# A four-part sequence network on one core: the scan's sum over states by accumulated transposes, exp/ln table loads placed after planning, and a re-planned issue order

## Chip, cores and metric

The kernel runs on one core of one Trainium2 chip. The metric is the device time of one execution in microseconds (us). The kernel before takes 1695.54 us (median of 3 runs, 1694.59 to 1696.02).

## What is computed

Eight sequences of 256 tokens with 128 features go through six stages: a gated linear recurrence, local attention with a gated feed-forward block (two layers) and a selective scan ("mamba"), a mixture of 32 experts, a block of chunked attention and feed-forward layers, a mixture of 8 experts, and a last attention layer with a ternary linear map. All of it is float32, each stage with residual and normalisation. The part that the change rewrites is the selective scan, cut to its core:

```python
xz = x @ W_in;  x_inner, z = jnp.split(xz, 2, axis=-1)
xc = silu(causal_conv(x_inner));  x_ssm = xc @ W_xproj      # delta, B (16 states), C (16 states)
delta = softplus(x_ssm[..., :1] * w_dt + b_dt);  A = -exp(A_log)
# h_t = exp(delta*A) * h_(t-1) + delta*B*xc ;  y = sum over the 16 states of h * C
y = selective_scan(xc, delta, A, B, C) + xc * D_param
out = (y * silu(z)) @ W_out
```

## The kernel before

Activations lie with the 128 features on the partitions and tokens along the free axis. `_Kernel` emits the six stages as Python generators, stage by stage: `rglru`, `local_mamba`, `moe1`, `chunked`, `moe2`, `typed`. What sets the order of the work is `_Order`, at the very end: it takes all instructions and their dependencies, runs a list scheduler over five queues (PE, ACT, DVE, POOL, SP) with a table of durations (`LENGTHS`: time until the queue is free, time until the result is there), and in `impose` chains every queue in the order found. A ready instruction is chosen by its rank, which is its place in the program plus an entry of the table `BIAS` (by queue, tile and stage). `STAY` is a handicap for an instruction that needs another ACT table set or another PE tile shape than the one before. So a change in an instruction, in a duration or in a bias can move instructions on all queues in all stages.

**The scan of one sequence** (`mamba_sequence`, L1216 to L1327). The 256 inner channels are two halves `c` of 128 partitions. PE makes `xin` and `z`; ACT applies Silu to `z` (tile `sz`, L1244) and, after DVE's convolution, to `xc` (L1245). Then come `xps`, a broadcast row `raw`, ACT's softplus steps (L1273 to L1276), and POOL (DVE in the last sequence) makes `e`, `r`, `d` and `u = d*xc` (L1280 to L1284). Eight steps `m` follow, each with two of the 16 states:

- SP loads the rows of B and C, spread over the partitions (`bc`, L1262); ACT makes four `da = exp(d*na)` (L1295);
- DVE makes `hs = u*B` (L1297), scans it in place (L1299) and multiplies it by C (L1300), each over 128x1024 elements;
- PE adds both states' halves up in one PSUM bank `y` by two matmuls with the identity as weights and 128x512 moving columns (L1303). On this line the trace lists the helper `mm`, L863; each float32 matmul leaves two records.

After the eighth step DVE adds `xc*D` from PSUM (L1306, two instructions), POOL multiplies by `sz` (L1307, tile `t`; DVE in the last sequence), PE multiplies by `wout`, and a layer normalisation and the router's logits follow. Four local-attention sequences and two scans are in flight together. When the last scan runs there is nothing left beside it but the folding of later weights and the routing of the first 14 token tiles.

**The routing of `moe1`** (`route1`, L1468 to L1536) runs once for token tiles 0 to 13, which need sequences 0 to 6, and once for tiles 14 and 15. Its DVE steps end in `put` (L1512), the row numbers. After that POOL scatters each tile's 128 rows to DRAM by an indirect DMA (L1616, 14 and then 2). SP and ACT read the sorted rows back (`got`, L1636) when all 16 scatters have landed, and only then has PE work for the experts.

**ACT table sets.** Exp and Ln share a set; Sigmoid, Gelu and Silu need others. `exp_ln` (L891 to L897) emits an explicit load of the Exp/Ln set in the program, after the last Gelu or Silu of a block, and `keep` ties it to its place. The planner handles that load as an instruction. Where an activation finds another set, the compiler adds a load ahead of it; the trace lists such a load on the activation's own line, and the explicit ones at L893.

Of the kernel before, what the change touches and what calls it, by code (L numbers as in the profile page):

```python
# [23 lines left out]
P = 128  # L24
# [285 lines left out]
class _Order:  # L310
# [12 lines left out]
    STAY = dict(PE=70, ACT=310)  # L323
    BIAS = {
        "ACT  1": 495, "ACT  3": -495, "ACT d 2": -1445, "ACT e 4": -700, "ACT e 6": 370, "ACT fh 4": -30, "ACT four 4": 630, "ACT four 5": -345,
        "ACT ge 2": 385, "ACT got 3": 50, "ACT got 5": 590, "ACT k 2": -275, "ACT kp 4": -40, "ACT lakq 2": -75, "ACT lavp 2": -95, "ACT lg 2": 620,
        "ACT lnrs 1": 225, "ACT lnrs 2": -280, "ACT lnsq 2": 40, "ACT ot 6": 75, "ACT ptsb 2": -740, "ACT qsq 2": -5, "ACT r 2": -70, "ACT rg 1": -590,
        "ACT rg 2": -320, "ACT rn 2": 55, "ACT rs 4": -50, "ACT rs 6": -25, "ACT s 6": -190, "ACT savp 2": -5, "ACT sg 3": 560, "ACT sh 5": -250,
        "ACT spl 1": -410, "ACT spt 1": -15, "ACT st 6": 460, "ACT v 2": 25, "ACT xc 2": -2725, "ACT xchunked 2": -400, "ACT xchunked 4": -390,
        "ACT xs 2": 10, "ACT xsq 4": -660, "DVE ab 4": 720, "DVE bt 3": -1225, "DVE bt 5": 190, "DVE centre 0": -205, "DVE d 2": -10,  # L330
        "DVE decaypart 4": -240, "DVE e 2": 50, "DVE four 5": 105, "DVE fs 4": 10, "DVE gate 2": -345, "DVE gate 5": -320, "DVE get 2": 180, "DVE get 4": 5,
        "DVE get 5": 850, "DVE got 4": -40, "DVE h 2": 5, "DVE h 5": -525, "DVE hs 2": 5, "DVE k 5": -680, "DVE lares 2": -200, "DVE lg 4": 665,
        "DVE nm 2": -135, "DVE nm 6": -95, "DVE oh 2": -285, "DVE oh 4": 2440, "DVE oh 5": -180, "DVE ptsb 2": 20, "DVE ptsb 6": -250, "DVE put 2": 190,
        "DVE put 4": 480, "DVE q 5": 470, "DVE q 6": 785, "DVE r 2": -120, "DVE rc 2": -270, "DVE rc 4": 175, "DVE route 2": -345, "DVE s 2": 20,
        "DVE s 5": -95, "DVE s 6": 1585, "DVE sares 2": 30, "DVE sel 4": -50, "DVE sg 3": -250, "DVE sm 4": 365, "DVE spt 1": 810, "DVE st 6": 150,
        "DVE sum 2": -705, "DVE t 5": 400, "DVE th 4": 650, "DVE u 2": 255, "DVE vec 2": 50, "DVE we 4": -30, "DVE wlocal 2": 1325, "DVE xc 2": -1830,
        "DVE xla 4": -580, "DVE xlf 4": 75, "DVE xlocal 2": -860, "DVE xmoe 6": 10, "DVE xpf 4": -10, "DVE xrglru 2": 205, "DVE xsa 4": 485, "DVE ys 3": 100,
        "DVE z 4": -190, "PE a 2": 50, "PE acc 5": 10, "PE b 2": 30, "PE bt 3": 1010, "PE bt 5": -580, "PE cum 2": 80, "PE cum 4": -1270, "PE fold 2": 105,
        "PE g 2": -700, "PE gate 1": -345, "PE gate 2": 345, "PE hps 4": -15, "PE kps 4": 95, "PE lg 2": 205, "PE lin 6": -1140, "PE ln 1": 355,
        "PE ln 2": -45, "PE o 6": -910, "PE out 4": -35, "PE pg 5": -20, "PE proj 5": 100, "PE proj 6": -570, "PE ps 4": -455, "PE pt 2": -25,  # L340
        "PE pt 4": -125, "PE pu 3": 2550, "PE pu 5": -720, "PE py 3": 740, "PE qkt 2": -1425, "PE raw 2": -1360, "PE rows 2": 585, "PE sc 2": -60,
        "PE sc 4": 30, "PE sc 6": -1215, "PE v 5": 470, "PE v 6": -20, "PE vps 2": 1025, "PE vps 4": -10, "PE wo 2": 60, "PE wo 6": -855, "PE wout 2": -95,
        "PE xps 2": -790, "PE y 2": 20, "PE z 2": 40, "PE zt 4": -20, "POOL biasrows 3": -595, "POOL e 4": 415, "POOL e 6": -305, "POOL got 5": 490,
        "POOL km 5": 665, "POOL mean 0": 635, "POOL one 0": 395, "POOL places 2": -70, "POOL places 5": -240, "POOL q 5": 50, "POOL q 6": -325,
        "POOL rest 4": -990, "POOL rg 1": -25, "POOL rows 4": 85, "POOL ss 2": -20, "POOL t 2": 595, "POOL u 2": 110, "POOL zero 0": -35,
        "POOL zeros 1": -385, "SP bc 2": 200, "SP cst 3": -455, "SP got 3": 535, "SP got 5": 505, "SP outdram 6": 275, "SP places 1": 1460,
        "SP rottable 0": 45, "SP routetables 0": 495, "SP rows 4": -370, "SP scales 2": 40, "SP vec 0": -1475, "SP wattn 2": 15, "SP wmoe 2": -150,
        "SP wmoe 4": -150, "SP wmoe 5": -100, "SP xs 2": -660,
    }
    LENGTHS = {  # L350
        "ACT  LoadActFuncSet  ": (1178, 1283), "ACT d Ln 128x512 128x512": (544, 649), "ACT da Exp 128x255 128x255": (403, 508),
        "ACT e Abs 128x256 128x256": (460, 565), "ACT e Exp 128x128 128x128": (422, 527), "ACT e Exp 128x256 128x256": (460, 565),
        "ACT e Exp 128x512 128x512": (526, 631), "ACT four Exp 128x2 128x2": (98, 203), "ACT got DMACopy 128x512 128x512": (451, 3502),
        "ACT h TensorCopy 64x255 64x255": (295, 400), "ACT k TensorCopy 128x512 128x512": (484, 589), "ACT lnrs Exp 128x256 128x256": (317, 422),
        "ACT lnsq Square 128x256 128x256": (278, 383), "ACT ot TensorCopy 128x512 128x512": (490, 595), "ACT qsq Square 128x512 128x512": (498, 603),
        "ACT r Relu 128x256 128x256": (462, 567), "ACT rg Exp 128x1020 128x1020": (1039, 1144), "ACT rg Ln 128x1024 128x1024": (949, 1054),
        "ACT rn Exp 128x16 128x16": (111, 216), "ACT rn Ln 128x16 128x16": (116, 221), "ACT rs Exp 128x2 128x2": (97, 202),
        "ACT rs Ln 128x2 128x2": (98, 203), "ACT sh Silu 128x512 128x512": (492, 597), "ACT xc Identity 128x256 128x256": (465, 570),
        "ACT xc Silu 128x512 128x512": (524, 629), "ACT xchunked TensorCopy 128x256 128x256": (260, 365), "ACT xmoe Identity 128x256 128x256": (404, 509),
        "ACT xs TensorCopy 33x256 33x256": (255, 360), "ACT xsq Square 128x128 128x128": (296, 401), "DVE biaspart TensorCopy 96x256 96x256": (198, 283),  # L360
        "DVE decay TensorScalarPtr 128x512 128x512": (516, 601), "DVE decaypart TensorCopy 128x512 128x512": (334, 419),
        "DVE four TensorScalarPtr 128x4 128x4": (74, 159), "DVE ge TensorScalarPtr 128x256 128x256": (384, 469),
        "DVE ge TensorScalarPtr 85x256 85x256": (368, 453), "DVE h TensorTensor 128x256 128x256": (317, 402),
        "DVE hs TensorScalarPtr 128x1024 128x1024": (2191, 2276), "DVE hs TensorTensor 128x1024 128x1024": (1123, 1208),
        "DVE mv BNStatsAggregate 128x2 128x6": (85, 170), "DVE nm TensorTensor 128x8 128x8": (67, 152), "DVE ptsb TensorCopy 128x512 128x512": (594, 679),
        "DVE rc Reciprocal 128x16 128x16": (158, 243), "DVE rc Reciprocal 128x4 128x4": (83, 168), "DVE rc Reciprocal 128x8 128x8": (109, 194),
        "DVE rg TensorScalarPtr 128x256 128x256": (580, 664), "DVE rottable TensorScalarPtr 128x256 128x256": (260, 345),
        "DVE s TensorScalarPtr 128x128 128x128": (253, 338), "DVE s TensorTensor 128x256 128x256": (324, 409), "DVE st BNStats 128x6 128x128": (197, 282),
        "DVE sum TensorReduce 128x32 128x448": (736, 821), "DVE t TensorScalarPtr 128x256 128x256": (385, 470),
        "DVE t TensorTensor 128x512 128x512": (595, 680), "DVE vec TensorTensor 128x1 128x1": (60, 145), "DVE vec TensorTensor 85x1 85x1": (59, 144),  # L370
        "DVE vs TensorCopy 128x512 128x512": (594, 679), "DVE wlocal TensorScalarPtr 128x682 128x682": (483, 568),
        "DVE x TensorScalarPtr 128x256 128x256": (369, 454), "DVE xc TensorScalarPtr 128x254 128x254": (384, 469),
        "DVE xla TensorScalarPtr 128x256 128x256": (429, 514), "DVE xlocal TensorTensor 128x256 128x256": (310, 395),
        "DVE xpf TensorScalarPtr 128x256 128x256": (577, 662), "DVE z TensorScalarPtr 128x128 128x128": (292, 377),
# [62 lines left out]
    def group(self, i):  # L437
# [5 lines left out]
        if e == "ACT":  # L443
            return 1 if op == "LoadActFuncSet" else self.SETS.get(str(x.func).split(".")[-1]) if op == "Activation" else None
        return None

    def change(self, i):
        x, e, op = self.ops[i]
        if e == "ACT":
            return 0.0 if op == "LoadActFuncSet" else self.TABLE  # L450
# [120 lines left out]
    def length(self, i):  # L571
# [20 lines left out]
        if e == "ACT":  # L592
            if op == "LoadActFuncSet":
                return float(self.TABLE), float(self.TABLE)
# [1805 lines left out]
```

## Time and profile before

| what | before |
|---|---|
| median of 3 runs | 1695.54 us |
| the profiled execution, and the span of its trace | 1695.66 us, 1692.0 us |
| mean granted TensorE clock | 0.947 |
| PE, PE weight loads | 1442.4 us (85%), 932.5 us (55%) |
| DVE, ACT, POOL | 1138.2 us (67%), 976.5 us (58%), 579.2 us (34%) |
| ACT table loads | 74 of 1283 ns |

The span leaves out 3.66 us around the trace. A busy share is an average over six stages with different limits, so the profile is read here by windows of time: about 0 to 42 us is `rglru`, 42 to 800 us `local_mamba`, to 852 us the hand-over to `moe1` and `moe1` itself, to 1290 us `chunked`, to 1440 us `moe2`, to the end `typed`. The chain of waits is the sequence of work that ended last, followed back from the last instruction; "issue" is time in it in which an engine waited for nothing that the profile shows.

### The profile page before, as it was taken

What the parts mean: (1) busy time and instruction counts of PE and PEld (TensorE: products, weight loads), DVE (VectorE), ACT (ScalarE), POOL (GpSimd) and SP (SyncE); (2) the same over time, 40 slices, a digit from 0 to 9 for tenths busy, and PEclk for the clock granted to TensorE, in tenths of its full rate; (3) what the DMA queues carried; (4) which work ended last, traced back from release to release, by engine and by line L of the source; (5) the groups of instructions that cost most, each with busy time, mean ns of one, the idle gap of its engine ahead of it and who ended that gap; (6) DMA issues with size and microseconds to landing.
All of it is one profiled execution on the core that took longest, in us unless ns stands there. A gap on an engine that the chain in (4) does not pass through costs nothing.

```text
span 1692.0 us, 28693 instructions
## 1 busy us (share of the span) xinstructions
PE 1442.4 (85%) x10858; PEld 932.5 (55%) x10858; DVE 1138.2 (67%) x2182; ACT 976.5 (58%) x2661; POOL 579.2 (34%) x535
## 2 busy tenths in 40 slices
PE   2688897979788877676679999999997998999997
PEld 1355553545454544343557776766674764566664
DVE  5755579898989898689354656566445332588885
ACT  3777887787877868644135554545443222366654
POOL 1344462616263423100331222221214004567573
PEclk7799999999999998899789999999997998999998
DMA  5000012121212213266310000000102121000000
GB/s 193 1 1 1 1 39 63 39 63 39 63 39 63 64 38 97 66 196 242 111 47 2 8 14 11 7 8 5 46 2 68 47 82 30 18 5 4 8 4 10
DMA packets 45113, 77.97 MB, mean 46 GB/s; under 512 B 5580, under 2 KB 21988, under 8 KB 43824
## 3 DMA queue, kind: packets, MB, share of 16 engines
q1 hardware_dynamic: 39648, 70.02, 13.8%
q0 software_dynamic: 3216, 5.07, 1.1%
q8 instruction: 85, 1.39, 0.3%
q10 hardware_dynamic: 2112, 1.05, 0.2%
q14 instruction: 52, 0.43, 0.1%
HBM read 66.87 MB, written 10.76 MB: 46 GB/s over the span
## 4 chain that ended last, share of the span: by engine, by line
PE 49%; DVE 23%; ACT 11%; issue 9%; POOL 5%; DMA 2%; another core or an unknown queue 0%; SPq 0%; ACTq 0%; DVEq 0%; POOLq 0%
PE vps L863 7%; PE kps L863 6%; PE sc L863 5%; PE out L863 4%; DVE hs L1299 3%; DVE hs L1300 3%; PE pu L863 3%; PE pg L863 3%; PE pt L974 3%; DVE hs L1297 2%; PE o L863 2%; ACT e L1146 2%; PE hps L863 2%; PE py L863 2%; PE acc L863 2%
## 5 line engine op out<-in xcount | busy, mean ns | idle before, releaser
L863 PE MATMUL y<-hs,ident 128*128 128x512 f32 x256 | 136.7, 647 | 30.2 <-DVE hs L1300 29.9
L1151 POOL TENSOR_TENSOR e<-e,rc 128x1024 f32<-128x1024 f32 x32 | 79.6, 2486 | 228.3 <-DVE rc L1150 227.6
L1299 DVE TENSOR_TENSOR_SCAN hs<-da,hs 128x1024 f32<-128x1024 f32 x64 | 154.1, 2409 | 0.1
L2250 ACT ACTIVATE e<-sc,nm 128x128 f32<-128x128 f32 (+1 forms) x256 | 105.1, 426 | 64.1 <-DVE nm L2245 55.2
L974 PE MATMUL pt<-ident,e 128*128 128x128 f32 x768 | 119.2, 281 | 18.0 <-POOL e L1151 12.4
L1295 ACT ACTIVATE da<-d,na 128x255 f32<-128x255 f32 x256 | 110.5, 508 | 22.5 <-DVE hs L1299 20.2
L1146 ACT ACTIVATE e<-sc,nm,rn 128x128 f32<-128x128 f32 x256 | 114.7, 468 | 10.9 <-DVE nm L1141 10.5
L974 PEld LDWEIGHTS pt<-ident,e 128*128 128x128 f32 x768 | 88.4, 143 | 56.3 <-issue 19.2
L2253 POOL TENSOR_TENSOR e<-e,rc 128x1024 f32<-128x1024 f32 x48 | 91.1, 1897 | 65.6 <-DVE rc L2252 65.5
L1829 POOL TENSOR_TENSOR e<-e,rc 128x512 f32<-128x512 f32 x32 | 33.9, 1059 | 226.1 <-DVE rc L1828 173.4
L1098 POOL TENSOR_TENSOR t<-t,t 128x512 f32<-128x512 f32 x64 | 84.1, 1316 | 61.1 <-DVE t L1085 56.0
L1651 POOL DMA_INDIRECT got<-ybuf,get x48 | 45.7, 952 | 169.0 <-DMA ybuf<-ys 87.6
L1804 ACT COPY kp<-kps 128x512 f32<-128x512 f32 x128 | 74.8, 585 | 48.5 <-PE kps L863 46.7
L1297 DVE TENSOR_TENSOR hs<-u,bc 128x1024 f32<-128x1024 f32 x64 | 87.5, 1384 | 6.2 <-POOL u L1284 5.5
L863 PEld LDWEIGHTS y<-hs,ident 128*128 128x128 f32 x256 | 47.5, 204 | 77.9 <-DVE hs L1300 47.5
L1300 DVE TENSOR_TENSOR hs<-hs,bc 128x1024 f32<-128x1024 f32 x64 | 87.5, 1369 | 0.0
L863 PE MATMUL qk<-w_local,h 128*128 128x512 f32 x128 | 71.1, 644 | 13.0 <-DVE t L1085 6.2
L976 DVE COPY ptsb<-pt 128x512 f32<-128x512 f32 x104 | 69.0, 677 | 17.0 <-PE pt L974 16.0
L1840 ACT COPY vs<-vps 128x512 f32<-128x512 f32 x64 | 37.4, 584 | 67.5 <-PE vps L863 56.8
L863 PE MATMUL vps<-sa_vp,x_lf 128*32 128x512 f32 x512 | 69.8, 594 | 0.0
L976 ACT COPY ptsb<-pt 128x512 f32<-128x512 f32 x88 | 51.4, 584 | 31.3 <-PE pt L974 30.7
L2245 DVE TENSOR_REDUCE nm<-sc 128x4 f32<-128x1024 f32 (+1 forms) x48 | 58.3, 1215 | 15.2 <-PE sc L863 14.6
(380 smaller groups left out, 3800.0 us busy)
## 6 DMA issues: line engine op xcount, KB each, us to landing
bc<-xs SPq DMA_DIRECT2D x128, 256.0 KB
w_moe<-in_e_dram SPq DMA_DIRECT2D x16, 768.0 KB
w_attn<-in_w_dram SPq DMA_DIRECT2D x4, 1024.0 KB
w_local<-in_w_dram SPq DMA_DIRECT2D x2, 1557.0 KB
places<-zeros SPq DMA_DIRECT2D x2, 1280.0 KB
got<-places SPq DMA_DIRECT2D x6, 256.0 KB
ybuf<-ys SPq DMA_DIRECT2D x8, 160.0 KB
x_in<-in_x_dram SPq DMA_DIRECT2D x1, 1024.0 KB
```

Of the source, the lines that this page charges most:

```text
L863: return self.nc.tensor.matmul(out, lhsT, rhs, start=start, stop=stop)
L974: self.last = self.nc.tensor.transpose(pt[:, j * P : (j + 1) * P], src[:, j * P : (j + 1) * P], self.ident)
L976: copy(sb.rearrange("p a b -> p (a b)"), pt)
L1098: nc.gpsimd.tensor_add(t1, t1, t2)
L1146: nc.scalar.activation(e[:, j, g, :], scs[:, j, g, :], AF.Exp, bias=nm[:, j, g : g + 1], scale=rq[:, j, g : g + 1], accum_out=sm[:, j, g : ...
L1151: nc.gpsimd.tensor_tensor(e, e, rc.unsqueeze(3).to_broadcast([P, 2, 4, P]), ALU.mult)
L1295: nc.scalar.activation(da[:, n, c, 1:S], d[:, c, 1:S], AF.Exp, scale=na[:, i : i + 1])
L1297: nc.vector.tensor_tensor(hs, u.unsqueeze(1).to_broadcast(shp), bn, ALU.mult)
L1299: nc.vector.tensor_tensor_scan(line(hs), line(da), line(hs), 0.0, ALU.mult, ALU.add)
L1300: nc.vector.tensor_tensor(hs, hs, cn, ALU.mult)
L2250: nc.scalar.activation(e[:, i, :], sc[:, i, :], AF.Exp, bias=nm[:, i : i + 1], accum_out=sm[:, i : i + 1])
L2253: nc.gpsimd.tensor_tensor(e, e, rc.unsqueeze(2).to_broadcast([P, n, keys]), ALU.mult)
```

## The change

- **Sum over states.** Each 128x512 identity matmul becomes four 128x128 PE transposes that accumulate in the PSUM bank, so `y` now has tokens on the partitions. Accordingly `z` is made with tokens on the partitions, `xc*D` is made on POOL (in place, after `u`) and enters the sum as four more transposes, one DVE instruction multiplies `y` by `sz`, four transposes (`yg`) turn the product back and ACT copies it to SBUF for `wout`. Over the kernel 128 matmuls become 544 accumulating transposes and 32 ordinary ones.
- **Table loads.** `exp_ln` and `keep` go, and so does the preload of the Silu set in `route1`. The planner plans without loads; when its order is found, one load of the Exp/Ln set is put directly ahead of each Exp or Ln that follows another set.
- **Row writes and gathers.** The planner's duration for an indirect DMA on POOL goes from 995 (`places`) and 949 (`got`) to 1280 ns.
- **The plan.** All `LENGTHS` entries are renewed, `BIAS` is another table throughout, `STAY` goes from PE 70, ACT 310 to PE 140, ACT 720.

```diff
-    STAY = dict(PE=70, ACT=310)
+    STAY = dict(PE=140, ACT=720)
...
-        "POOL got DMACopy 128x128 2560x128": (949, 2493),
-        "POOL places DMACopy 2560x128 128x128": (995, 2277),
+        "POOL got DMACopy 128x128 2560x128": (1280, 2500),
+        "POOL places DMACopy 2560x128 128x128": (1280, 2500),
...
     def impose(self):
         order, _ = self.plan()
+        ring, last = [], None
+        for i in order["ACT"]:
+            g = self.groups[i]
+            if g is not None:
+                if g == 1 != last:
+                    load = self.tc.nc.scalar.preload_act_table_set("natural_log_exp_and_others")
+                    self.ops.append((load.ins, "ACT", "LoadActFuncSet"))
+                    ring.append(len(self.ops) - 1)
+                last = g
+            ring.append(i)
+        order["ACT"] = ring
...
-            for c in range(2):
-                self.mm(ps[:, c * S : (c + 1) * S], win[:, 256 + c * P : 256 + (c + 1) * P], x)
+            for t in range(2):
+                self.mm(ps[:, t * S : (t + 1) * S], x[:, t * P : (t + 1) * P], win[:, 256:512])
             sz = tile("sz", 2)
             nc.scalar.activation(flat(sz), ps, AF.Silu)
-            self.exp_ln(nc.scalar.activation(xc, xc, AF.Silu))
+            nc.scalar.activation(xc, xc, AF.Silu)
...
+            nc.gpsimd.tensor_tensor(xc, xc, self.v("dpar", 0, 2).unsqueeze(2).to_broadcast([P, 2, S]), ALU.mult)
         yield 3.0
-        yp = self.psum("Y", "y")
+        yp = self.psum("Y", "y").rearrange("p (t c d) -> p t c d", t=2, c=2)
+
+        def gathered(src, first, last):
+            for c in range(2):
+                for t in range(2):
+                    self.nc.tensor.matmul(
+                        yp[:, t, c, :], src[:, c, t * P : (t + 1) * P], self.ident, start=first and c + t == 0, stop=last and c + t == 2, is_transpose=True
+                    )
...
             for n in range(2):
-                self.mm(yp, self.ident, flat(hs[:, n]), m == 0 and n == 0, m == 7 and n == 1)
+                gathered(hs[:, n], m == 0 and n == 0, False)
             yield 2.3
-        yg = tile("t")
+        gathered(xc, False, True)
+        nc.vector.tensor_tensor(flat(sz), yp.rearrange("p t c d -> p (t c d)"), flat(sz), ALU.mult)
+        ps = self.psum("M", "yg")
         for c in range(2):
-            nc.vector.scalar_tensor_tensor(yg[:, c, :], xc[:, c, :], self.v("dpar", c), yp[:, c * S : (c + 1) * S], ALU.mult, ALU.add)
-        eng.tensor_mul(yg, yg, sz)
+            for t in range(2):
+                nc.tensor.transpose(ps[:, c * S + t * P : c * S + (t + 1) * P], sz[:, t, c * P : (c + 1) * P], self.ident)
+        nc.scalar.copy(flat(sz), ps)
         ps = self.psum("M", "wout")[:, 0:S]
         for c in range(2):
-            self.mm(ps, wout[:, c, :], yg[:, c, :], c == 0, c == 1)
+            self.mm(ps, wout[:, c, :], sz[:, c, :], c == 0, c == 1)
```

The other hunks drop the calls of `exp_ln` and `keep` (in `rglru_group`, `local_block`, `local_mamba`, `route1`, `moe1`, `moe2`, `typed_weights`) and the planner's cases for a load.

How the order of the instructions moves, from the two built kernels: ACT has 62 table loads instead of 74. Up to the second recurrence group in `local_mamba` there are 8 instead of 13, in the rest of `local_mamba` 48 instead of 55, and 6 in both after that. On DVE, the `put` of the 14 tiles stands behind the last scan and directly ahead of the last `hs` product before; after, DVE still has 3 scans, 5 `hs` products and 3 short routing steps between `put` and the end of the last `hs` product, and behind that product, ahead of the multiplication by `sz`, four routing steps of the 14 tiles and one step of a later weight. ACT's new copy of `sz` stands between the next sequence's convolution start (`xc`, Identity) and its Silu, or directly behind that Silu. In the last two sequences the Exp/Ln load stands after the Abs and Relu of the softplus and ahead of its Exp, where before it followed the Silu directly.

## The prediction

> **What bounds the kernel.** I read the page's first two parts, then busy time by windows, the chain of waits in order of time, and single rows. The page's shares and the matmul group that the change removes:
>
> ```profile
> PE 1442.4 (85%) x10858; PEld 932.5 (55%) x10858; DVE 1138.2 (67%) x2182; ACT 976.5 (58%) x2661; POOL 579.2 (34%) x535
> ...
> L863 PE MATMUL y<-hs,ident 128*128 128x512 f32 x256 | 136.7, 647 | 30.2 <-DVE hs L1300 29.9
> ```
>
> PE leads on average, and the sum over states takes 136.7 us of it. But all of it lies in `local_mamba`, so its worth is read there. The columns after the length are busy us (and counts) of PE, weight loads, DVE, ACT, POOL, then the clock:
>
> ```profile
> 296.00:381.00 85.00, 73.89 (x463) 43.74 (x460) 76.03 (x96) 68.36 (x182) 36.81 (x34) 1.00 0.18 51
> ...
> 634.00:821.00 187.00, 125.68 (x560) 69.00 (x559) 146.63 (x181) 102.78 (x233) 39.91 (x36) 0.87 0.45 138
> 852.00:1290.00 438.00, 412.99 (x4599) 300.31 (x4600) 246.92 (x796) 208.00 (x495) 97.30 (x107) 0.97 0.05 14
> ```
>
> In steady state DVE has 76 of 85 us (89%), PE 87%, ACT 80%: three engines near full, DVE ahead. In the tail (634 to 821) DVE leads again. `chunked` is PE's alone (94%), and nothing there is removed. The chain from 300 to 634 says the same, DVE's scan steps first:
>
> ```profile
> by line: issue 11.6%; DVE hs L1300 10.9%; DVE hs L1299 9.7%; DVE hs L1297 7.3%; DVE nm L1140 3.8%; POOL e L1151 3.2%; PE qk L863 2.9%; POOL t L1098 2.9%; POOL h L1062 2.5%; ACT e L1146 2.4%; DVE ge L1204 2.3%; PE qkt L1103 2.0%; PE o L863 2
> ```
>
> So PE time saved here is worth only what of it stands in that chain. I added up the chain's pieces from 127 to 821: all of PE's are 110 us of 694, those of `y` 8.2 us.
>
> **1. Transposes for matmuls.** The rows: one step's two matmuls, and eight transposes at the same clock.
>
> ```profile
> 744.08 1.98 PE L863 MATMUL y<-hs,ident 128*128 128x512 f32 x4 [1.13 <-DVE hs L1300]
> ...
> 1307.27 1.04 PE L1643 MATMUL bt<-ident,got 128*128 128x128 f32 x8
> ```
>
> 64 steps at 1.04 are 66.6 us; the four transposes of `xc*D` and four of `yg` per sequence add 8 x 1.04 = 8.3. PE falls by 136.7 - 66.6 - 8.3 = 61.8 us, 11% of its 558 us between 127 and 821. Lower bound of its worth: the chain's own `y` pieces shrink by 1 - 1.04/1.98 = 47%, 3.9 us. Upper: all of PE's chain pieces shrink by 11%, 12.2 us. I take **-8**, the middle, because the other matmuls wait behind `y` in one queue, while DVE at 89% takes back part.
>
> No row shows transposes that accumulate. If they ran like ordinary matmuls (`wout`, 128x256 at 404 ns a record, two records), PE would gain nothing; that is a rival below.
>
> The Trainium skill speaks against the row: "TensorE: Matmul & The Clock Gate", Part 4, says that the fast clock does not engage for transpose mode, which does not count as busy. In this trace transposes among matmuls run at the full clock (the 1.04 us above), but with PE idle before, the same eight took 1.94 us at 825. By the page this part would bring 0 in place of -8.
>
> The rest of the edit: DVE loses two instructions of 0.468 us and gains one of 0.69, nothing. POOL trades one product of 1.27 us for one of 1.19 (row of `t<-t,rn`, which also has a spread factor), behind `u` and ahead of nothing that waits. ACT gets 8 copies of 0.585, 4.7 us, paid by the loads below. `z` is the same pair of 512-column products.
>
> From a sequence's last `hs` product to `wout` the path was 5.2 us at 744 (two matmuls 2.0, two DVE steps, POOL 1.27). Now it is 12 transposes 1.56, DVE 0.69, four transposes 0.63, ACT 0.59 and four handovers of 0.1: 3.9. That is -1.3, and it counts twice, where nothing else runs beside it (691 and 749): -2.6.
>
> **2. Table loads.** 12 loads less, 15.4 us of ACT. Where they count:
>
> ```profile
> 49.41 1.28 ACT L1013
> 50.71 0.69 ACT rg L1013
> 51.41 1.28 ACT L1091
> 52.71 0.22 ACT rn L1091
> 52.92 0.48 ACT q L1104
> 53.40 0.50 ACT qsq L1078
> 53.92 1.28 ACT L1092
> 55.21 0.21 ACT rn L1092
> 55.44 1.28 ACT L1013
> ```
>
> From 45.5 to 65 us eight loads stand in the chain; after the change four are left there, -5.1 at most, nothing at least, since DVE is at 78% from 42 to 85 and is late next. I take half, **-2.6**. A fifth (17.59) lies under DVE's scans. Of the 55 loads (70.6 us) in the rest of `local_mamba` 16.5 us stand in the chain, 23%; seven less are 9.0 us, so **-2.1** (0 to -9.0).
>
> In the last two sequences the load now follows the softplus' Relu. Before it ran while ACT waited for PE (748.56, followed by that wait). Now it is in line: 2 x 1.28 = +2.6, which just cancels the shorter path above. **Together 0.**
>
> The skill's "ScalarE: Activation LUTs", What ACT_TABLE_LOAD costs, adds a drain of about 1.38 us to each load. The rows above show none: load at 49.41, next activation at 50.71. By the page the two terms would double, to about -9.
>
> **3. Row writes.** POOL's scatters of the first 14 tiles:
>
> ```profile
> 799.48 1.32 POOL L1616 DMA_INDIRECT places<-x_chunked,put  x1 [50.34 <-DVE get L1523]
> 801.11 0.99 POOL L1616 DMA_INDIRECT places<-x_chunked,put  x1 [0.30 <-issue]
> 802.40 0.97 POOL L1616 DMA_INDIRECT places<-x_chunked,put  x1 [0.30 <-issue]
> ```
>
> They are 1.28 us apart (0.97 plus 0.30), and POOL was idle for 50 us before. The last two tiles' `put` came at 813.43, yet their scatters queued until 819.24, and `got` went out at 821.44, 21.6 us after the last `hs` product (799.80). In the new order `put` precedes that product's end by 3 scans and 5 products, about 12.5 us (2.2 and 1.12 apart in the tail). The 14 end near +5.5. The second `put` is late by 1.0 us: 2.6 us of short steps (0.61, 0.88, 0.62, 0.28, 0.24) now stand on DVE ahead of the product by `sz`, where 1.56 us of transposes would be the wait; with 0.69, 0.63, 0.59 and three handovers of 0.1 `wout` starts at +4.8, before at +3.84. So `put` at +14.6 in place of +13.6. Two scatters, 0.9 after it, start at +15.5 and +16.8; `got` follows 2.2 later, at +19.0. **-2.6.** The other side: if 14 scatters beside DVE slow its products as a POOL product does (1.13 to 2.46 us at 544), 5 x 1.3 = 6.6 worse, +4.0 in all. The gathers in later stages issue in the same queue places but for a few; nothing.
>
> **4. The new order elsewhere.** Work in `chunked`, `moe2` and `typed` is the same, and PE holds 94% of `chunked`. A shuffle can move their idle time both ways: PE idles 12 us of 84 from 1269 to 1353 and ACT and PE stand for 6.4 us at 1404. Value **0**, bounds -8 to +8.
>
> **Sum**, against the profiled execution: 1695.66 - 8 - 2.6 - 2.1 + 0 - 2.6 = 1680.4 us. The profiled execution lies 0.12 above the median, which shifts nothing: **1680.4**.
>
> **Rivals.**
>
> *DVE hides it.* DVE keeps its work; if PE's relief is all waiting for DVE, only parts 2 and 3 remain: 1695.66 - 7.3 = 1688.4. For it: 89% DVE and its lead in the chain. Against: 62 us of "issue" between 212 and 634, which PE's queue partly causes. The transposes not being faster ends here too.
>
> *The order repairs more.* With three engines under 90%, their waits for each other are the loss: 10% of 338 us on DVE from 296 to 634. Halved, that is -17 in place of the -8 of part 1, so 1671.4; with half of the later stages' bound (-4) 1667.
>
> *Slower: ACT's new copy blocks its queue.* `sz<-yg` stands ahead of the next sequence's Silu, `xs` and `da`. It waits for the transposes, a DVE product and four transposes, up to 3.9 us, where the waiting product before sat on POOL, 34% busy. It also holds one of two PSUM banks "M". Eight sequences at 3.9 are 31 us: 1680.4 + 31 = 1711. It decides from 15.3/8 = 1.9 us of stall a sequence. Against: DVE has the product by `sz` ahead of two convolution steps (0.47 each) that the Silu needs anyway.
>
> **Chances.** Forecast 0.50 (1680.4, own range 1673 to 1689), DVE hides 0.20, repairs more 0.16, blocked ACT 0.14. About 0.2% (3.4 us) is what a measurement can tell from no change. Faster: 0.48 + 0.14 + 0.16 = 0.78; same: 0.01 + 0.05 + 0.02 = 0.08; slower 0.01 + 0.01 + 0.12 = 0.14. The range takes in DVE's case with a bad shuffle and most of the repair: 1661 to 1699.
>
> **What would show it.** Right: `y` near 70 us of PE busy time; PE about 80% and DVE above 91% from 296 to 634; four loads between 45 and 62; first scatter ahead of the last scan's end and `got` 19 us after the last product; `local_mamba` shorter by some 12 us, `chunked` unchanged. Wrong: transposes of `y` above 0.2 us each or a clock below 0.95 in steady state; DVE idle unchanged; ACT idle before `sz<-yg` above 1.9 us a sequence; a later stage that moved by more than 8 us.

## The result and the profile after

The changed kernel takes 1707.3 us (median of six runs, 1702.3 to 1709.2), the kernel before beside it on the same chip 1695.8 (1693.9 to 1698.1): ratio 1.0062, 95% interval 1.0053 to 1.0072. Predicted were 1680.4 us and faster; it became some 11 us slower. Measured again later on another chip the ratio was 1.0071 (1.0047 to 1.0095), with 1676.0 us for the kernel before. So times are compared here only as ratios to the kernel before on the same chip.

The profile after (execution of 1708.73 us), its shares and the group of the sum:

```profile
PE 1429.1 (84%) x11178; PEld 975.7 (57%) x11178; DVE 1145.2 (67%) x2173; ACT 964.5 (57%) x2657; POOL 585.3 (34%) x536
...
L1286 PE MATMUL y<-ident,hs 128*128 128x128 f32 x512 | 86.7, 319 | 33.4 <-DVE hs L1303 33.1
```

The sum lost 50 us of PE busy time, yet PE as a whole lost only 13. The busy times by windows tell where the rest went (columns as before: PE, PEld, DVE, ACT, POOL, clock):

```profile
296.00:381.00 85.00, 70.89 (x498) 47.10 (x498) 73.70 (x95) 66.88 (x179) 39.94 (x34) 0.96 0.18 51
...
634.00:821.00 187.00, 120.13 (x676) 87.67 (x677) 145.70 (x154) 101.18 (x233) 45.03 (x34) 0.74 0.44 138
852.00:1290.00 438.00, 415.96 (x4631) 297.45 (x4629) 241.99 (x743) 204.86 (x477) 93.60 (x103) 0.97 0.05 14
```

`chunked` (852 to 1290) has the same work at the same clock. In the tail (634 to 821) the granted clock fell from 0.87 to 0.74. In the steady state DVE, the engine that was to be kept busier, has 73.7 of 85 us where it had 76.0. The head of the chain from 300 to 634 has another face too; `hs` was three of the first four entries with 28%, now it is 18% (L1300, L1302, L1303) and an ACT step leads:

```profile
by line: ACT e L1141 7.9%; DVE hs L1302 7.7%; issue 7.1%; DVE hs L1300 5.2%; DVE hs L1303 4.8%; ACT da L1298 3.1%; POOL t L1093 2.7%; PE ln L873 2.7%; PE qkt L1098 2.5%; ACT L759 2.5%; POOL xc L1279 2.4%; POOL e L1146 2.3%; PE vps L873 2.3%
```

I added up the chain's pieces from 127 to 821 us for both kernels, without "issue". Before: DVE 243, ACT 131, PE 113 us, with 11 whole table loads (14.1 us). After: DVE 195, ACT 189, PE 152, with **24 whole table loads (30.8 us)**. In a second pair of profiles it was 13 and 20 loads. So the count moves by a few from one execution to the next, but in both pairs the change has twelve loads fewer and more of them on the path.

Milestones, as the difference after minus before in us (second column: both profiled once more, on the second chip):

| milestone | first | second |
|---|---|---|
| first scan starts | -6.8 | -2.7 |
| output of sequence 1 / 3 / 5 / 7 / 8 | -1.4 / -0.5 / +2.4 / +8.0 / +10.2 | +3.8 / +5.4 / +7.0 / +14.8 / +15.5 |
| PE's first work on the sorted rows | +6.4 | +11.2 |
| end of `chunked` | +12.1 | +13.4 |

An early gain, a loss that grows through `local_mamba`, and some 4 us given back in the row writes. What is lost after that differs between the two executions, 5.6 us in `chunked` in the one, 2.2 in the other; with one execution each I leave it at that.

### The profile page after: what moved, and what is told of

Same layout as the page of the kernel before. It is cut to its first block, busy times and chain, and to the rows that moved or that the text cites. A ratio compares the mean times of both kernels' runs of the same rounds, so it can differ in the third digit from the quotient of the medians.

```text
span 1706.7 us, 29313 instructions
## 1 busy us (share of the span) xinstructions
PE 1429.1 (84%) x11178; PEld 975.7 (57%) x11178; DVE 1145.2 (67%) x2173; ACT 964.5 (57%) x2657; POOL 585.3 (34%) x536
## 4 chain that ended last, share of the span: by engine, by line
PE 52%; DVE 19%; ACT 14%; issue 7%; POOL 5%; DMA 1%; ACTq 0%; SPq 0%; DVEq 0%; POOLq 0%
PE vps L873 8%; PE kps L873 6%; PE sc L873 6%; PE out L873 4%; PE pt L970 3%; ACT e L1141 3%; PE pu L873 3%; PE pg L873 3%; DVE hs L1302 3%; PE o L873 3%; DVE hs L1303 2%; DVE hs L1300 2%; PE hps L873 2%; PE py L873 2%; PE acc L873 2%
## 5 line engine op out<-in xcount | busy, mean ns | idle before, releaser
L1302 DVE TENSOR_TENSOR_SCAN hs<-da,hs 128x1024 f32<-128x1024 f32 x64 | 149.1, 2339 | 0.1
L1298 ACT ACTIVATE da<-d,na 128x255 f32<-128x255 f32 x256 | 108.7, 504 | 15.4 <-DVE hs L1302 13.1
L1286 PE MATMUL y<-ident,hs 128*128 128x128 f32 x512 | 86.7, 319 | 33.4 <-DVE hs L1303 33.1
L1286 PEld LDWEIGHTS y<-ident,hs 128*128 128x128 f32 x512 | 71.4, 166 | 50.8 <-DVE hs L1303 43.6
L1300 DVE TENSOR_TENSOR hs<-u,bc 128x1024 f32<-128x1024 f32 x64 | 91.7, 1448 | 2.1 <-POOL u L1278 2.0
L1303 DVE TENSOR_TENSOR hs<-hs,bc 128x1024 f32<-128x1024 f32 x64 | 85.1, 1338 | 0.0
L1839 DVE COPY vs<-vps 128x512 f32<-128x512 f32 x64 | 43.8, 684 | 40.7 <-PE vps L873 37.6
```

The costliest lines, as they stand in the source:

```text
L1286: self.nc.tensor.matmul(yp[:, t, c, :], src[:, c, t * P : (t + 1) * P], self.ident, start=first and c + t == 0, stop=last and c + t == 2, ...
L1298: nc.scalar.activation(da[:, n, c, 1:S], d[:, c, 1:S], AF.Exp, scale=na[:, i : i + 1])
L1300: nc.vector.tensor_tensor(hs, u.unsqueeze(1).to_broadcast(shp), bn, ALU.mult)
L1302: nc.vector.tensor_tensor_scan(line(hs), line(da), line(hs), 0.0, ALU.mult, ALU.add)
L1303: nc.vector.tensor_tensor(hs, hs, cn, ALU.mult)
```

## The experiments

The theories, as the expectations name them (where a run's expectation gives a letter another meaning, that one holds for the run). **A**: transposes do not hold the PE clock up. **B**: the newly planned order costs, the transposes themselves gain. **C**: DVE covers PE either way. Later **D**: the clock follows how busy PE is, whatever it does. **R**: the new ranks make a worse order for any work. **L**: late table loads cost. **F**: ranks fit one set of instructions and no other. **N**: only the order counts.

### The changed kernel, one thing undone at a time

`e1_sum_by_matmul`, with the same issue order on all five engines:

```diff
-    yp[:, t, c, :], src[...], self.ident, start=..., stop=..., is_transpose=True
+    yp[:, t, c, :], src[...], self.ident, start=..., stop=...
```

> The changed kernel, only that the 544 pieces summed into the bank y are matmuls against the identity (the same result, the same issue order on all five engines) instead of transposes. Theory A (transposes don't keep the PE clock up, and the lost clock stretches the other matmuls): PE does more work, since a 128x128 matmul is 0.23 us (row py of before) where the transpose was 0.142 planned, about +45 us of busy time at full clock; yet the granted clock between 212 and 761 us comes back from 0.88 to 0.69 into 0.92 to 1.00 as in the kernel before, and the time falls from 1707 to about 1699 (1693 to 1703). Theory B (the new issue order costs, the transposes are a gain): PE is 84% busy, 45 us more of it costs at least a fifth, 1715 or more, and the clock matters little. Theory C (PE is covered by DVE either way): within 2 us of 1707.

`e2_early_loads` (in `impose`):

```diff
-                    ring.append(len(self.ops) - 1)
-                last = g
+                    ring.insert(place, len(self.ops) - 1)
+                last, place = g, len(ring) + 1
```

> The changed kernel, only that each load of the Exp/Ln table stands directly behind the last Gelu, Silu or Sigmoid instead of directly ahead of the next Exp or Ln; the other four engines' order is the same. The chain of waits of the changed kernel shows two such loads of 1.28 us (at 701.4 and 759.8 us) on the path. Theory A (clock): the loads are a small part of the loss, 1.5 to 3 us come back, 1704 to 1706. Theory B (the late loads are what costs in the sequences): at least 6 us come back, 1701 or less. Theory C: PE is late anyway, within 1 us of 1707.

`e4_old_ranks_from_chunked` (the number in a key is its stage):

```diff
-    BIAS = {...}   all of the change
+    BIAS = {...}   of the change where the number is below 4, of before from 4 on
```

> The changed kernel, only that from the chunked stage on the planner's ranks (BIAS) are those of the kernel before; up to there the issue order is the same. In the profile, chunked took about 5 us longer in the changed kernel than before. Theory A (clock in local_mamba loses some 12 us against the early gain, and the re-planned chunked some 5 more): 1702 to 1703, with the start of the chunked stage unmoved. Theory B (the ranks later on cost nothing, those 5 us are the chip's scatter between executions): within 2 us of 1707. Theory C (the old ranks don't fit the changed costs): 1710 or more.

`c_before` and `c_after` are the two kernels unchanged, on the chip of the three runs above.

> The kernel before, again, for its profile on the chip of the three runs beside it. Every theory: its own time, within 0.3% of the other runs of it on this chip.

> The changed kernel, again, as the yardstick on the chip of the runs beside it. The lone load moved early gained nothing that the first call could show, and the sum by matmuls stood 4.6 us above it, so the transposes are worth about 3 to 5 us of this kernel. Every theory: 1.005 to 1.010 of the kernel before.

Measured, as ratios to the kernel before on one chip: changed kernel 1.0071 (1.0047 to 1.0095), sum by matmuls 1.0116 (1.0100 to 1.0132), early loads 1.0098 (1.0070 to 1.0126), old ranks 1.0406 (1.0388 to 1.0424). In the changed order the transposes are thus worth some 0.45% (0.2 to 0.7% by the two intervals), 6 to 8 us; A, which has them lose, falls. C has them worth nothing and falls for this order. B asked for 8 us or more, which the medians just miss. Early loads gain nothing that these runs can tell, so A and B of that run fall; that the planner arranged the order around the late loads would explain it, but no run shows that. Old ranks in the later stages cost 3.3%, far more than any part is worth: that was theory C of that run, by which the old ranks don't fit.

### Does a transpose hold the clock?

`m1_clock` runs PE alone. Its body is loops over these instructions:

```python
mm = lambda: nc.tensor.matmul(acc[:, 0:S], ident, x[:, 0:S], start=True, stop=True)
tr = lambda c: nc.tensor.matmul(acc[:, c*P:c*P+P], x[:, c*P:c*P+P], ident, start=True, stop=True, is_transpose=True)
im = lambda c: nc.tensor.matmul(acc[:, c*P:c*P+P], x[:, c*P:c*P+P], ident, start=True, stop=True)
```

> Computes nothing of the reference: PE alone, f32, in phases, each timed by its windows: 130 matmuls 128x256; 500 transposes 128x128; 130 matmuls; 250 matmuls 128x128 against the identity; then 25 rounds each of 6 matmuls and 4 transposes; 6 matmuls and a short ACT copy that PE waits for; 6 matmuls, 4 transposes, copy; 6 matmuls, 4 identity matmuls, copy; 6 matmuls, 4 transposes, 2 bf16 matmuls 128x256, copy; last 6 rounds of 25 matmuls, 20 transposes, copy. Theory A (transposes don't keep the clock up): in the phase of transposes the granted clock falls to 0.5 to 0.7, a transpose takes 0.22 us or more, and the mixture with transposes and copies stands below that with copies alone and below that with identity matmuls. Theory B (they count as work): the clock is 0.95 or more in the dense phases, a transpose takes 0.12 us, and the mixtures differ by their gaps alone.

The windows of its phases (PE busy, clock): matmuls; transposes; matmuls; identity matmuls; matmuls and transposes mixed.

```profile
30.00:64.00 34.00, 34.00 (x159) 1.00 0.00 0
66.00:118.00 52.00, 52.00 (x479) 1.00 0.01 1
120.00:174.00 54.00, 54.00 (x252) 1.00 0.00 1
176.00:230.00 54.00, 54.00 (x486) 1.00 0.00 1
232.00:306.00 74.00, 74.00 (x392) 1.00 0.00 1
```

500 transposes took 54.75 us (0.11 us each) at a clock of 1.00, 250 identity matmuls of the same size 55.99 us (0.22 each). The first mixtures with short ACT copies in between (310 to 385 and 390 to 474 us, PE 91% busy) stood at 1.00 as well. These are the figures of theory B. So in this run a float32 transpose cost half of the identity matmul and kept the clock. The sinking clock of the changed kernel needs another cause; `m2_paced_bursts` paces PE by DVE, as the tail does:

```python
for _ in range(18):
    src = ring.tile([P, 2048], F32, tag="src", name="src")      # two buffers
    nc.vector.tensor_scalar(src, x, 1.0, None, ALU.add)
    nc.vector.tensor_scalar(src, src, 1.0, None, ALU.add)
    burst()                                                     # of PE, reads src
```

> Computes nothing of the reference: DVE works without a pause in steps of two operations 128x2048, and behind each step PE gets one burst, 18 steps a phase. The phases: 4 matmuls 128x512; 2; 8 transposes 128x128; 2 matmuls; 8 matmuls 128x128 against the identity; 1 matmul; 8 transposes and 8 bf16 matmuls 128x256 in turns; 16 transposes; 2 matmuls. Theory D (the clock follows how busy PE is, whatever it does): the granted clock of the 8 transposes is that of the 1 matmul (about the same 0.9 us of work) and below that of the 2 matmuls, and the 16 transposes have that of the 2 matmuls. Theory A (transposes do not hold the clock): 16 transposes have a lower clock than 2 matmuls, and a transpose takes 0.22 us or more.

Windows inside the phases: 2 matmuls a step; 8 transposes; 1 matmul; 16 transposes.

```profile
100.00:138.00 38.00, 31.39 (x64) 10.84 (x64) 37.45 (x33) 0.00 (x0) 1.00 0.00 0
143.00:190.00 47.00, 27.32 (x133) 23.65 (x132) 38.53 (x33) 0.00 (x0) 0.61 0.00 0
...
280.00:320.00 40.00, 23.21 (x28) 6.61 (x28) 32.69 (x28) 0.00 (x0) 0.67 0.00 0
...
368.00:420.00 52.00, 42.55 (x336) 35.95 (x334) 51.25 (x45) 0.00 (x0) 1.00 0.00 1
```

This is theory D: the 8 transposes (0.61) stand near the single matmul (0.67), the 16 transposes with the two matmuls (1.00). Of the other phases, 4 matmuls, 2 matmuls and 8 identity matmuls had 1.00; transposes and bf16 matmuls in turns had 0.87, as they began at half clock and had 1.00 from 337 us on. The timeline shows what tells the phases apart, in the brackets: 0.4 us of idle time between bursts of 2 us held the clock, 2.5 us did not. (In the two slow phases DVE took two steps together, so their bursts are 16 transposes or two matmuls, 1.8 us at full clock.) A burst of two matmuls, one of 16 transposes, one of two matmuls:

```profile
120.00 1.98 PE L326 MATMUL acc<-src,ident 128*128 128x512 f32 x4 [0.41 <-DVE src L368]
...
165.13 3.68 PE L329 MATMUL acc<-ident,src 128*128 128x128 f32 x16 [2.46 <-DVE src L368]
...
305.63 2.95 PE L326 MATMUL acc<-src,ident 128*128 128x512 f32 x4 [2.45 <-DVE src L368]
```

What PE did in a burst made little difference; less work in a stretch that another engine paced meant longer gaps, and with them a slower clock for all that PE did there. Gaps between 0.4 and 2.5 us were not tried, and the length of the gaps is not told apart from PE's busy share (82% in the fast phases shown, 58% in the slow ones).

### The parts in the old order

The parts planned alone would each get a new order. These kernels keep the old one: every engine issues its instructions in the sequence of the kernel before, and only the part itself differs (in e8 and e10 the pieces of a sum were planned as one instruction of the old duration).

`e8_transposes_in_old_order`; its sums are transposed in blocks, all later work is as before:

```diff
-                self.mm(yp, self.ident, flat(hs[:, n]), m == 0 and n == 0, m == 7 and n == 1)
+                for q in range(4):   
+                    nc.tensor.matmul(yp[:, q*P:q*P+P], flat(hs[:, n])[:, q*P:q*P+P], self.ident, ..., is_transpose=True)
```

> The kernel before in its own issue order on all five engines, with each of the 128 summing matmuls 128x512 replaced, in its place, by four transposes 128x128 into the same bank (the blocks come out transposed, so what follows computes on transposed blocks; every other instruction is as before). This is the first part of the change without a new order. Theory B (the re-planned order is what costs; the transposes are a gain): 5 to 9 us below the kernel before, as PE loses 128 x 1.07 us of matmul for 512 x 0.11 us of transposes, some 62 us or more, of which DVE covers most. Theory D (PE now idles more, the granted clock falls in the stretches that DVE sets, and the other matmuls take the gain back): within 3 us of the kernel before or above it, and the clock between 634 and 846 us falls from 0.84 to 0.92 to below 0.80.

`e10_more_pe_in_old_order` keeps that matmul and adds the four transposes behind it:

```diff
+                for q in range(4):
+                    nc.tensor.matmul(yp[:, q*P:q*P+P], flat(hs[:, n])[:, q*P:q*P+P], self.ident, ..., is_transpose=True)
```

> The kernel before in its old order, with each summing matmul 128x512 followed by four transposes of the same blocks into the same bank (so the sums are wrong by those blocks): 512 x 0.11 us = 56 us more for PE in the local_mamba stage. If DVE and ACT set the pace there (the rival of the prediction in which DVE hides the matmuls): 1.000 to 1.004. If PE sets the pace or its clock does: the same 0.23 us by 256 steps that the prediction put on the path, 8 us and more, 1.005 or more.

`e13_less_dve_in_old_order`:

```diff
-            nc.vector.tensor_tensor(hs, hs, cn, ALU.mult)
+            nc.vector.tensor_tensor(hs[:, :, :, 0:P], hs[:, :, :, 0:P], cn[:, :, :, 0:P], ALU.mult)
```

> The kernel before in its old order, with the last of DVE's three operations on hs done on the first half of the columns only (the second half is summed without its factor): 64 x about 0.55 us = 35 us less for DVE in the local_mamba stage, as much as the transposes took from PE. If DVE sets the pace there: 12 us or more below the kernel before (0.993 or less), seen in the times at which each sequence ends. If neither does and the waits run round through all engines: 0.998 to 1.000, as with the transposes.

Transposes for matmuls: **1.0000 (0.9991 to 1.0010)**. 56 us more of PE as planned (its busy time rose by 46, 1442 to 1489): 1.0033 (1.0019 to 1.0047). 32 us less of DVE (1138 to 1106): **0.9850 (0.9835 to 0.9864)**, 25.5 us. Windows 296 to 634 and 634 to 821, the kernel before on e8's chip:

```profile
296.00:634.00 338.00, 286.06 (x1674) 169.30 (x1674) 302.80 (x370) 266.80 (x686) 150.26 (x129) 0.98 0.20 51
634.00:821.00 187.00, 131.35 (x561) 70.65 (x559) 146.55 (x179) 102.94 (x233) 38.91 (x35) 0.85 0.44 138
```

and e8:

```profile
296.00:634.00 338.00, 266.69 (x1804) 178.28 (x1803) 301.68 (x371) 266.39 (x684) 151.40 (x130) 0.96 0.20 51
634.00:821.00 187.00, 120.53 (x652) 87.28 (x650) 146.05 (x178) 101.71 (x230) 38.90 (x35) 0.73 0.44 138
```

PE lost 30 us in the two (35 in the whole kernel: 54 of the sum, of which the other matmuls took 19 back at the lower clock), DVE, ACT and POOL did what they did before. The outputs of sequences 2 to 5 came 1.5 to 1.7 us ahead of the kernel before, the lead that e8 already had ahead of its first transpose (1.4 to 2.0). The chain's `y` pieces from 127 to 821 fell from 19 to 0.9 us, and DVE's rose from 239 to 289: what left PE was late on DVE at once. The head of e8's chain from 300 to 634:

```profile
by line: issue 12.8%; DVE hs L1300 11.3%; DVE hs L1299 10.5%; DVE hs L1297 8.0%; DVE nm L1140 3.9%; POOL t L1098 2.9%; DMA bc<-xs 2.3%; DVE ge L1204 2.2%; PE qk L863 2.1%; ACT qsq L1078 1.9%; ACT e L1146 1.9%; PE ln L863 1.9%; DVE ss L1079 
```

In the tail the clock went to 0.73, as in the changed kernel. The last output came 0.6 us behind the kernel before, but PE's first work on the sorted rows 1.7 us ahead again: what the clock may have cost there did not last. In e10 the tail's clock rose to 0.91, with more to do, as theory D has it:

```profile
634.00:821.00 187.00, 145.68 (x769) 90.96 (x764) 146.57 (x175) 104.93 (x237) 35.95 (x32) 0.91 0.43 138
```

With DVE relieved (e13) the chain passed to ACT: 204 us of it, where the kernel before had 131, and DVE 159.

`e9_late_loads_in_old_order` plans with the old loads, then takes them out and puts one ahead of each Exp or Ln behind another set, as the change does; `e9b` puts it directly behind the last function of the other set; `e9c` puts it where the kernel before had a load, if it had one there:

```diff
# e9, in impose of the kernel before
+        for i in order["ACT"]:
+            if i is an old load: continue
+            if g == 1 != last: ring.append(load)
# e9b
-            if g == 1 != last: ring.append(load)
+            if g == 1 != last: ring.insert(behind the last of the other set, load)
# e9c
+            if i is an old load and last != 1 and place is None: place = len(ring)
+            if g == 1 != last: ring.insert(len(ring) if place is None else place, load)
```

> The kernel before with every instruction in its old order on all five engines, but the table loads taken out after planning and put directly ahead of the first Exp or Ln behind another function: 62 loads in place of 74, 15.4 us less of ACT. This is the second part of the change without a new order. The prediction's second term: about 5 us less, 0.997. Theory N (only the order counts; ACT has slack wherever a load goes): 0.999 to 1.001. Theory L (late loads stand on the path of the scans): 1.003 or more.

> As the run beside it, but each of the remaining 61 loads directly behind the last Gelu, Silu or Sigmoid instead of directly ahead of the Exp or Ln. Theory N: as the run beside it, within 0.1%. Theory L, and the prediction's remark on exposed loads: 2 us or more below the run beside it.

> The kernel before in its old order, where the table loads that no Exp or Ln used are gone (62 for 74), and each load that is needed stands where the kernel before had one, directly ahead of its Exp or Ln only where it had none. Theory L (late loads cost, fewer loads gain what lies on the path): 0.997 to 0.9995, faster than both kernels. Theory N (ACT has slack where the spare loads stood): 0.9995 to 1.001. If still 1.002 or more, the old places too were hiding something that is not the load.

| kernel, old order | loads | of them in the chain, 127 to 821 | ratio (95%) |
|---|---|---|---|
| before | 74 | 11 and 13 (14.1 and 16.7 us, two executions) | 1 |
| e9, late | 62 | 17 (21.8 us) | 1.0057 (1.0042 to 1.0072) |
| e9b, early | 61 | 13 (16.6 us) | 1.0024 (1.0012 to 1.0035) |
| e9c, old places | 62 | 8 (10.2 us) | 0.9983 (0.9972 to 0.9995) |

Theory L holds in all three, N in none. The number of loads hardly differs in the last three; their places do, and the time follows. The count in the chain points the same way for e9 and e9c; e9b's 13 is within what the kernel before shows, and with DVE relieved (e13) 27 loads stood in the chain of a faster kernel, so it compares only kernels with the same work. Of e9's 17, twelve are the late ones: two ahead of the softplus of the last two sequences, ten ahead of an attention step (`rn` or `e`). e9's chain at the softplus of sequence 7, and e9c's (the kernel before has the same pieces there as e9c):

```profile
703.57 0.46 ACT r L1306
...
704.04 1.28 ACT L776
...
705.34 0.63 ACT e L1307
```

```profile
695.22 0.46 ACT r L1308
695.67 0.52 ACT e L1309
```

In the old place the load ran while ACT waited for PE (`xps`, in e9c's chain from 691.53 to 692.56):

```profile
691.22 1.28 ACT L778 ACT_TABLE_LOAD   x1
```

Placed late, it waits for its turn and then everything waits for it. e9c, with 15 us less of ACT, is 0.17% faster than the kernel before and so faster than both: the best here that computes the same, and only just.

### One part, planned anew

e6 is the changed kernel with the old `mamba_sequence`, but without `exp_ln`; x4 is e6 with the old tables of the planner; e5 is the kernel before with the new `mamba_sequence`, with `exp_ln` and the new durations of its forms; x3 and x12 exchange the ranks:

```diff
# x3, in the kernel before (x12: the other way round, in the changed kernel)
-    STAY = dict(PE=70, ACT=310)
+    STAY = dict(PE=140, ACT=720)
-    BIAS = {...}   the table of before
+    BIAS = {...}   the table of the change
```

> The changed kernel with the old sum (128 matmuls against the identity and the old steps behind the scan); loads, spacing and ranks as changed, and planned anew. Theory B (the order under the new ranks costs): 1.010 or more of the kernel before, at or above the sum by matmuls in the changed order (1.0116). Theory D (the thinner PE work costs, the rest gains): 0.995 to 1.000, as parts two and three give some 7 us.

> The kernel before with the planner's BIAS and STAY of the changed kernel, nothing else: the same work, the same early loads, planned anew. Theory R (the new ranks make a worse order whatever the work): 1.007 or more. Theory L (the late loads are what costs): within 0.3%. Theory F (ranks fit one set of instructions and no other): 1.01 or more, and the next three runs are slower than the kernel before as well.

> The kernel before with the table loads left out of the plan and put directly ahead of the first Exp or Ln behind another function, under the ranks and STAY of before. Theory R: within 0.3% or faster. Theory L: 1.005 or more, with DVE's waits for ACT in the local_mamba stage grown by 8 us or more. Theory F: 1.005 or more, with the waits spread over other steps.

> The kernel before with the transposed sum and its new steps behind the scan, planned anew under the ranks, STAY and early loads of before. The prediction's first term: 8 us less, ratio 0.995. Theories R and L: 0.998 to 1.000, as in the old order the transposes gained nothing. Theory F: 1.005 or more.

> The changed kernel with BIAS and STAY of before: sum, loads and spacing as changed. Theory R: within 0.3% of the kernel before, or faster. Theory L: 1.005 to 1.010. Theory F: above the changed kernel's 1.007.

| kernel | work | loads | ranks, STAY | ratio (95%) |
|---|---|---|---|---|
| changed | new | late | new | 1.0071 (1.0047 to 1.0095) |
| e6 | old | late | new | 1.0178 (1.0155 to 1.0201) |
| x3 | old | old | new | 1.0448 (1.0426 to 1.0470) |
| x4 | old | late | old | 1.0162 (1.0127 to 1.0197) |
| e5 | new | old | old | 1.0193 (1.0170 to 1.0216) |
| x12 | new | late | old | 1.0397 (1.0360 to 1.0435) |

This fits theory F: each kernel between the two is slower than both, by 1 to 4%. Theory R fails on x4, e5 and x12, theory L on x3, e5 and x12. That each table of ranks was tuned to its own kernel is inferred from this; no run shows how they came about. A new plan also changes the number of loads (87 in x3, 78 in e5, 64 in x4 and x12), since each change of table set in the order needs one. So such runs measure the new order, not the part; that is why the runs in the old order were needed.

## Why the prediction was wrong

**Part 1, the step that failed first:** "I take **-8**, the middle, because the other matmuls wait behind `y` in one queue". PE lost less than predicted (136.7 us became 86.7 for the steps and 10.8 for the new transposes, 39 of the predicted 62; the pieces ran at 0.17 us in place of 0.13, at the lower clock), but that is not the reason: in the old order the worth is 0 within 1.7 us (e8), below my lower bound of 3.9. (Added up again, the `y` pieces of the chain are 10.7 us and not 8.2, which would make that bound 5.) The bound took the `y` pieces out of the chain as if nothing were late next. It was DVE, at 89 to 90% in the same view: e13 shows 80% of a DVE saving in the time, e10 some 12% of a PE cost. The rival "DVE hides it" was right on this part. In the changed order, where the chain has more of PE, the same transposes save 6 to 8 us (e1), but against an order that was worse to begin with; that this is near my 8 is chance.

The Trainium skill's "TensorE: Matmul & The Clock Gate", Part 4, by which this part would bring 0, had the right number. Its reason, that transposes do not count as busy in the same way, is not what the runs show in float32: 1.00 through 500 of them, and at 16 a step as with two matmuls. The measurement decides. That the clock sank because PE had less to do between its waits for DVE fits m2 and e10; in e8 it sank with no change but the transposes.

**Part 2:** "12 loads less, 15.4 us of ACT" came true, and of eight loads in the chain near 50 us four were left, as said (47.63, 50.28 with 0.17 us of it, 53.70, 56.76); the first scan started 2.7 to 6.8 us earlier for 2.6 predicted. The step that failed is "seven less are 9.0 us, so **-2.1**": it took the same share of the path for loads that stand elsewhere. In the old order the late placing costs 9.6 us (7.1 to 12.2; e9) where I had -4.7. I had seen the mechanism at the softplus of the last two sequences (+2.6, two exposed loads); in e9 it also holds at the attention steps, ten of the twelve late loads in the chain. In the chain of the changed kernel, load and last sequence's end:

```profile
701.41 1.28 ACT L759
...
759.78 1.28 ACT L759
761.07 0.63 ACT e L1269
761.70 0.47 ACT x_chunked L1507
...
807.26 2.82 PE y L1286 x12
...
810.87 1.13 PE yg L1312 x4
```

The last two lines also show the size of the shorter path: 12 transposes were to take 1.56 us and took 2.82 at half clock, four 1.13 for 0.63. The gain of 1.3 us at the end of the tail was gone: from the last `hs` product to the last output it took 12.3 us where it was 9.5 (9.8 and 8.7 in the second pair).

**Part 3:** the mechanism was right, the size differs by execution. The first scatter came ahead of the last scan's end (805.93), and `got` went out 20.7 us after the last `hs` product where it was 21.6, predicted 19.0: -0.9 for -2.6.

```profile
795.61 2.36 POOL L1616 DMA_INDIRECT places<-x_chunked,put  x1 [28.78 <-DVE route L1527]
...
827.90 1.49 SPq L1636 DMA_DIRECT2D got<-places  x3
```

The second `put` came 16.3 us after that product, not 14.6, with those slow transposes ahead of it. In the second pair `put` came at 13.4 and `got` 17.8 us after the product where it was 21.7, -3.8. That the first five scatters now run 2.3 us apart beside DVE's `hs`, and not 1.28, cost nothing: POOL was idle for 6.2 us ahead of the last two.

**Part 4:** "Value 0" for the new order was the largest omission, but for `local_mamba`, not the later stages. There the changed kernel lost 15.5 us on the second chip, the transposes none. Late loads by themselves make 9.6 in the old order; in the changed order moving them early brought nothing back (e2), so the split between them and the other moved instructions stays open. What the second pair of profiles shows of it: before, DVE's longest waits were for the softplus (`t<-e`, 18.5 us between 250 and 800 us); after, for the attention of the following sequences (`x<-wo` 13.7, `h<-ln_rs` 12.9).

Of the rivals, ACT's copy did not block: 5.6 us of idle time ahead of it in all eight sequences together, where 1.9 each was the limit. "The order repairs more" had the sign wrong. None of my rivals had the loads as the slower side, although two loads that are "in line" (+2.6) were in my own sum.

## What to carry to other kernels

Before a saving on one engine is counted, ask in the same view which engine is late next, and test it by taking as much from that one: 32 us off DVE gave 25.5, 35 off PE gave 0. A table load that ran in another engine's wait cost nothing, and moved to the last moment it became a cost even with fewer of them: ask which loads stand in the chain, not how many the kernel has. Where a planner makes the order, hold it fixed when a part is measured: planning anew moved the time here by 1 to 4%, more than any part.

## What the runs showed of the hardware

A float32 128x128 transpose took 0.11 us back to back, the identity matmul of the same size 0.22, and both held the granted clock at 1.00. Bursts worth some 1.8 us with 2.5 us of idle time between them brought it to 0.61 (transposes) and 0.67 (matmuls); bursts of 2 us with 0.4 us between them left it at 1.00. Which of the two matters, the gap or PE's busy share (58% and 82%), is open. A table load took 1283 ns in every kernel profiled, and the next activation could follow 0.01 us behind it.
